# A decoder layer on one core: the first norm's result turned in blocks on VectorE and carried through DRAM instead of turned on TensorE

## The chip, the cores and the metric

The kernel runs on one core of a Trainium2 chip. The core has five engines that each work through their own queue in order: TensorE (PE, matrix products), VectorE (DVE), ScalarE (ACT), GpSimd (POOL) and SyncE (SP, which here only issues DMAs). The metric is the time of one execution on the device in microseconds (us); lower is better. Everything is computed in float32.

## The reference, cut to what matters

The input has 16 sequences of 512 tokens with 256 features. For each sequence the reference computes an attention layer and a feed-forward layer, each followed by a residual addition and a layer norm without gain.

```python
q = query @ wq + query @ Aq @ Bq * LORA_SCALE
k = query @ wk
v = query @ wv + query @ Av @ Bv * LORA_SCALE
# 16 heads of 16; rope on q and k; causal softmax of q k / 4; out = attn @ v
x = _layernorm(x + out @ wo)                     # the first norm
h = x @ W_exp + b_exp                            # 256 -> 1024, the expansion product
h = butterfly(h, up_weights, 1024)               # ten stages, linear
h = gelu(h + up_bias, approximate=False)
h = butterfly(h, down_weights, 1024)             # ten stages, linear
x = _layernorm(x + h @ W_con + b_con + down_bias)  # the second norm
```

The butterflies are linear, so the kernel folds them into the two weight matrices once, at the start.

## The kernel before, in words

A sequence is cut into four tiles of 128 tokens; the features into two chunks of 128. The heads of a chunk are worked on in groups, even and odd ones apart, which gives four "quads" for each sequence: (chunk 0, even), (chunk 0, odd), (chunk 1, even), (chunk 1, odd). Each quad takes five slots, so a sequence takes 20 slots (`per = 20`). A slot is the unit of the order written out by hand: for each slot the program emits first the attention work of the slot, then a list of other work (`others[s]`), then a list of work for the end of the slot (`holes[s]`). Every engine's queue has its instructions in exactly this order; nothing is reordered later.

The attention work of a slot. Two passes run over the scores, 15 slots apart. The first pass (`largest`, L421 on PE and L430 on DVE) computes scores and finds the largest of each row; the second (`weights`, L479 on PE, L493 on ACT and L497 on POOL) computes transposed scores with that maximum taken off, applies Exp on ACT and zeroes the masked part on POOL. In each slot PE computes score products of both passes into two score banks, pb and pa, of which there is one each: the next slot's score products may only write a bank when its readers are done. In slots of kind 0 to 3 (the slot's number modulo 5) pb holds the Exp's scores and pa the maxima's. In kind 4 each bank holds half of both: on pb the Exp is emitted before the maxima, on pa the maxima before the Exp. After the scores, PE multiplies finished weights with the values (`weigh`, po, L521) in slots of kind 0, 2 and 4; then come the others of the slot.

For the sequence that starts at slot s = 20 b, the other work lies at these slots (counted from s; slot 40 + n of one sequence is slot n of the sequence two later):

- load_xT at 0, load_x (the residual input z) at 9
- projections of the next sequence's q and k (`project`, pqk, L337) in the hole of slot 10, four products of 1.8 us each; their swap DMAs; rope on POOL (`turn`) and a copy with rows masked on ACT (`part`) in the slots after
- values (`project_v`, pvv, L383) at -3, -1, 4 and 14, the copy on ACT
- the division by the softmax's sums (`normalize`, L553 and L554 on DVE) at 27 to 31 and 36 to 40
- output projection (`project_out`, pwo, L559) at 41 and 42, with the residual addition (L567) and the norm's statistics (L577, L578) on DVE
- first norm: `spread` at 42 (L589 on DVE, then a power on POOL, L590), `offset` at 43 (L595 on DVE), `centre` at 44 (four ACT instructions, L602, z = z * scale + offset)
- `turn_x1` at 45: eight 128x128 transposes on PE (pt, L616), two copies to SBUF on DVE (x1T, L617), and the addition of the output biases to z on POOL (L621)
- expansion product (`hidden`, ph, L633) at 46 to 49, two of eight chunks a slot, copied out by ACT (L646) or DVE (L644)
- the Gelus of all eight chunks (`gelus`, L651) at the head of the hole of slot 50, between two loads of ACT's function table (Exp and Gelu use different tables), while PE works on the projections of slot 10 of the later sequence
- contraction (`contract`, py, L660) in eight halves at 51, 52, 53, 55, 56, 58, 60, 63, each second half followed by the residual addition (L668) and statistics on DVE
- second norm: `spread` at 63, `offset` at 67, `centre` at 68, store of the result at 68.

The attention's second pass of a sequence runs at its slots 15 to 34. The last two sequences have orders of their own, and sequence 13 has its last two hidden chunks in slot 50 with Gelu applied straight from PSUM. In slots 2 to 44 the folding of the butterflies runs beside the attention as a list of small tasks. z tiles are in three buffers, x1T in one, h in one. SP's queue takes the DMAs in order; an issue that waits for a semaphore holds up those behind it. The lines that carry the first norm's way from z to x1T:

```python
pt = bank(f"pt1_{b}_{c}", [P, NT, P])
for t in range(NT):
    nc.tensor.transpose(pt[:, t, :], zs[b][:, t, c * P : (c + 1) * P], ident)
nc.vector.tensor_copy(
    state["x1T", b][:, c, :], pt.rearrange("p t q -> p (t q)")
)
```

## Time and profile before

| what | value |
|---|---|
| median of 3 runs | 1359.33 us (1358.64 to 1360.84) |
| the profiled execution's own time | 1357.15 us |
| its span, first to last instruction | 1355.4 us |
| PE busy | 1320.3 us (97%) |
| DVE busy | 925.8 us (68%) |
| ACT busy | 707.3 us (52%) |
| POOL busy | 510.9 us (38%) |
| granted TensorE clock | 0.993 |

In the lines of a timeline the first number is the start in us from the span's start, the second the duration (of all, where several are merged: x8), then the engine, the line of the kernel, the operation, and output<-inputs. What stands in brackets at the end is how long the engine had been idle before, and what it waited for. In a table of stretches the busy time of PE, PE's weight loads, DVE, ACT and POOL stand in this order, then the granted clock. In the groups by line, the numbers after the bar are the busy time of all together and the mean ns of one; pipelined matmuls overlap, so that their sum of durations is larger than their busy time.

### The profile page before, as it was taken

The numbers are of one execution on the slowest core, as the hardware profiler recorded it, in microseconds if no ns is written. First come the engines' busy times: TensorE is split into PE (matmuls) and PEld (weight loads), VectorE is DVE, ScalarE is ACT, GpSimd is POOL, SyncE is SP. The second block draws the span as 40 slices with busy tenths as digits, with TensorE's granted clock in tenths as the row PEclk, the third lists the DMA queues.
The fourth block names the chain that finished last, engine by engine and source line by source line (L and its number), as shares of the span: only waits on it lengthen the run. The fifth ranks groups of instructions, "written<-read, shape, count | busy, mean of one in ns | idle before, by whom it ended". The sixth has DMA issues, their size and how long they took to land.

```text
span 1355.4 us, 23859 instructions
## 1 busy us (share of the span) xinstructions
PE 1320.3 (97%) x8728; PEld 702.5 (52%) x8728; DVE 925.8 (68%) x2949; ACT 707.3 (52%) x1079; POOL 510.9 (38%) x777
## 2 busy tenths in 40 slices
PE   8898999999999999999999999999999999998998
PEld 4453545455454545555454554545555454554555
DVE  4788757667685766758577685857768685776632
ACT  2575454454646445464645545464554546445643
POOL 3534215344251533425153352515335252531311
PEclk9998999999999999999999999999999999999999
DMA  5311010110102011010110101010110101000000
GB/s 172 120 45 45 22 59 30 40 45 30 68 30 74 30 41 45 30 67 30 67 35 31 57 30 68 30 60 30 40 60 30 68 30 55 30 27 32 30 12 31
DMA packets 45685, 63.49 MB, mean 47 GB/s; under 512 B 5752, under 2 KB 26232, under 8 KB 45568
## 3 DMA queue, kind: packets, MB, share of 16 engines
q1 hardware_dynamic: 41680, 56.42, 11.8%
q10 hardware_dynamic: 3888, 5.55, 1.3%
q8 instruction: 69, 1.13, 0.3%
q14 instruction: 48, 0.39, 0.1%
HBM read 23.40 MB, written 8.91 MB: 24 GB/s over the span
## 4 chain that ended last, share of the span: by engine, by line
PE 84%; DVE 11%; ACT 3%; issue 2%; DMA 0%; POOLq 0%; POOL 0%; DVEq 0%; SPq 0%; ACTq 0%
PE pb L479 19%; PE ph L633 17%; PE py L660 16%; PE po L521 10%; PE pqk L337 8%; DVE junk L430 5%; PE pvv L383 4%; PE pwo L559 3%; PE pa L421 3%; DVE bn L577 1%; PE pb L421 1%; PE pt L616 1%; ACT pT L493 1%; PE pa L479 1%; DVE z L567 1%
## 5 line engine op out<-in xcount | busy, mean ns | idle before, releaser
L430 DVE CUSTOM_DVE_ANT_0 junk<-pa,causal 128x384 bf16<-128x384 f32 (+2 forms) x878 | 438.3, 499 | 235.0 <-PE pa L421 176.1
L493 ACT ACTIVATE pT<-pb 128x1024 f32<-128x1024 f32 (+1 forms) x314 | 293.8, 936 | 377.3 <-PE pa L421 227.6
L497 POOL TENSOR_SCALAR_AFFINE_SELECT pT<-pT 128x256 f32<-128x256 f32 x512 | 202.5, 407 | 733.3 <-ACT pT L493 731.6
L479 PE MATMUL pb<-qz,kz 17*128 17x512 f32 (+2 forms) x1756 | 328.8, 473 | 16.1 <-ACT pT L493 12.1
L421 PE MATMUL pa<-kz,qz 32*128 32x384 f32 (+3 forms) x1756 | 329.2, 474 | 4.2 <-DVE mx L430 4.2
L660 PE MATMUL py<-wdn,h 128*128 128x256 f32 x1024 | 252.1, 391 | 0.0
L479 PEld LDWEIGHTS pb<-qz,kz 17*128 17x128 f32 (+1 forms) x1756 | 142.9, 183 | 179.5 <-issue 82.2
L633 PE MATMUL ph<-x1T,yb 128*128 128x512 f32 x512 | 235.8, 604 | 0.0
L660 PEld LDWEIGHTS py<-wdn,h 128*128 128x128 f32 x1024 | 185.1, 189 | 72.2 <-issue 36.2
L521 PE MATMUL po<-pT,vaug 128*32 128x512 f32 (+3 forms) x2048 | 179.5, 446 | 0.0
L633 PEld LDWEIGHTS ph<-x1T,yb 128*128 128x128 f32 x512 | 92.4, 189 | 122.3 <-issue 97.6
L421 PEld LDWEIGHTS pa<-kz,qz 32*128 32x128 f32 (+1 forms) x1756 | 143.7, 184 | 13.6 <-DVE mx L430 11.2
L553 DVE RECIPROCAL sums<-sums 128x128 f32<-128x128 f32 x128 | 121.1, 946 | 0.0
L337 PE MATMUL pqk<-xT,wqk 128*128 128x512 f32 x256 | 118.5, 613 | 0.0
L646 ACT COPY h<-ph 128x512 f32<-128x512 f32 x84 | 49.2, 585 | 123.2 <-PE ph L633 123.2
L521 PEld LDWEIGHTS po<-pT,vaug 128*32 128x32 f32 x2048 | 47.1, 109 | 102.3 <-issue 78.2
L430 DVE DVE_READ_ACCUMULATOR2_ANT mx<- 128x1 f32 x1024 | 84.5, 82 | 0.0
L337 PEld LDWEIGHTS pqk<-xT,wqk 128*128 128x128 f32 x256 | 48.0, 194 | 61.9 <-issue 57.4
L365 POOL TENSOR_TENSOR swap<-swap,rope_sb 128x512 f32<-128x512 f32 x62 | 79.6, 1283 | 0.0
L602 ACT ACTIVATE z<-z,norm 128x256 f32<-128x256 f32 x128 | 66.7, 589 | 24.6 <-DVE norm L595 24.5
L668 DVE TENSOR_TENSOR z<-py,z 128x256 f32<-128x256 f32 x64 | 27.1, 423 | 74.1 <-PE py L660 73.9
L430 DVE CUSTOM_DVE_ANT_0 junk<-pb,causal 128x256 bf16<-128x256 f32 (+3 forms) x146 | 63.6, 436 | 17.3 <-PE pa L421 4.0
(91 smaller groups left out, 1334.2 us busy)
## 6 DMA issues: line engine op xcount, KB each, us to landing
xT<-in_xT SPq DMA_DIRECT2D x16, 512.0 KB
swap<-qz SPq DMA_DIRECT2D x64, 128.0 KB
swap<-kz SPq DMA_DIRECT2D x64, 128.0 KB
z<-in_x SPq DMA_DIRECT2D x16, 512.0 KB
sums<-x SPq DMA_DIRECT2D x64, 128.0 KB
out_y<-z SPq DMA_DIRECT2D x15, 512.0 KB
x<-x SPq DMA_DIRECT2D x32, 128.0 KB
early<-in_wexpT ACTq DMA_DIRECT2D x1, 1028.0 KB
```

The lines of the kernel that those rows point to most:

```text
L337: nc.tensor.matmul(pq, wqk[:, d, e : e + P], xTs[b][:, d, :], start=(d == 0), stop=(d == NC - 1))
L365: engine.tensor_tensor(swap, swap, rope_sb[:, 1, :], ALU.mult)
L421: lambda i=i, rows=rows, at=at, n=n, t=t, ps=ps: nc.tensor.matmul(ps[:, i, at : at + n], q[rows, par, t * P : n], k_[rows, par, 0:n], star ...
L430: lambda i=i, at=at, n=n, t=t, g=g, ps=ps: nc.vector.tensor_tensor_reduce(out=junk[:, 0:n], in0=ps[:, i, at : at + n], in1=causal[:, T - n ...
L479: lambda i=i, rows=rows, at=at, n=n, k=block, ps=ps: nc.tensor.matmul(ps[:, i, at : at + n], kt[rows, par, k * P : (k + 1) * P], qt[rows, ...
L493: nc.scalar.activation(pT[:, heads, 0:n], ps[:, :, at : at + n], AF.Exp)
L497: nc.gpsimd.affine_select(out=diag, in_=diag, pattern=[[0, 2], [1, P]], compare_op=ALU.is_ge, fill=0.0, base=0, channel_multiplier=-1,)
L521: nc.tensor.matmul(po[HG * g : HG * (g + 1), k * P : T], vaugs[b % 2][:, k, NG * c + g, first : first + HG], pT[:, g, at : at + n], start= ...
L553: nc.vector.reciprocal(sums[:, ts], sums[:, ts])
L602: nc.scalar.activation(zs[b][:, t, :], zs[b][:, t, :], AF.Identity, bias=norm[:, 2, t : t + 1], scale=norm[:, 1, t : t + 1],)
L633: nc.tensor.matmul(ph, wup[:, c, hc * P : (hc + 1) * P], state["x1T", b][:, c, :], start=(c == 0), stop=(c == NC - 1),)
L660: nc.tensor.matmul(py, state["h", b][:, hc, t * P : (t + 1) * P], wdn[:, hc, :], start=(hc == 0), stop=(hc == NHC - 1),)
```

## The change

For the 14 sequences but the last two, the first norm's result is no longer turned on PE. `centre` moves from slot 44 to slot 43, behind `offset`. In slot 44, ahead of the other work of that slot, `turn_x1_by_blocks` has DVE transpose z in blocks of 32x32 (four instructions of 128x256), writes the blocks to a DRAM tile by four DMAs of 128 KB (pieces of 512 bytes), and reads x1T back by one DMA of 512 KB; all five are issued by SP. In x1T the tokens are then in another order, so that `hidden` reads its moving operand through an access pattern of 16 runs of 32 columns. POOL's addition of the output biases moves to slot 47. `hidden` moves to 48 to 51, the Gelus and the projections that accompany them to the hole of slot 52 (12), the contraction to 53, 55, 56, 58, 60, 63, 65, 66, the second norm to 66, 68, 69 with the store at 70. The next sequence's rope and part steps move by two slots with the projections, load_x moves from 9 to 20, and `normalize` of chunk 0 from 27, 28, 29, 31 to 29, 30, 31, 33. Sequence 13 loses its two fused chunks; the last sequence's four pvv all go to its slot 12. The folding's tasks are spread up to slot 46 instead of 44.

```diff
+    def turn_x1_by_blocks(b):
+        blocks = ring2.tile([P, D // HG, NT, HG], F32, tag="blocks", name=f"blocks_{b}", bufs=1)
+        for t in range(NT):
+            nc.vector.transpose(blocks[:, :, t, :], zs[b][:, t, :])
+        turned = dram.tile([D // HG, HG, NG, P], F32, tag="turned", name=f"turned_{b}")
+        for n in range(NG):
+            nc.sync.dma_start(
+                turned[:, :, n, :].rearrange("f j k -> j f k"),
+                blocks[HG * n : HG * (n + 1)].rearrange("j f t i -> j f (t i)"),
+            )
+        x1T = ring2.tile([P, NC, T], F32, tag="x1T", name=f"x1T_{b}", bufs=1)
+        nc.sync.dma_start(x1T, turned.rearrange("(c f) j n k -> (f j) c (n k)", c=NC))
+        state["x1T", b] = x1T.rearrange("p c (n t i) -> p c t n i", t=NT, i=HG)
...
-                state["x1T", b][:, c, :],
+                state["x1T", b][:, c],
...
-            at = {1: (-16, -11, -13, -9), B - 1: (-1, 4, 10, 10)}.get(b, (-3, -1, 4, 14))
+            at = {1: (-16, -11, -13, -9), B - 1: (12, 12, 12, 12)}.get(b, (-3, -1, 4, 14))
...
-            at = {0: (2, 5, 7, 10), 1: (3, 6, 8, 11)}.get(b, (10, 10, 10, 10))
+            at = {0: (2, 5, 7, 10), 1: (3, 6, 8, 11)}.get(b, (12, 12, 12, 12))
...
-                    add(turning + (6 if i == 3 else 4) + step, part, b + 1, side, c, step)
-        add(s + 9, load_x, b)
+                    add(turning + (6 if i > 1 else 4) + step, part, b + 1, side, c, step)
+        add(s + 20, load_x, b)
...
-                at = (27, 28, 29, 31) if c == 0 else (36, 37, 39, 40)
+                at = (29, 30, 31, 33) if c == 0 else (36, 37, 39, 40)
...
             add(s + 43, offset, 1, b)
-            add(s + 44, centre, 1, b)
+            add(s + 43, centre, 1, b)
+        if b + 2 == B:
             for c in range(NC):
-                add(s + 45 + (b + 2 == B), turn_x1, b, c)
+                add(s + 45, turn_x1, b, c)
         if b + 2 < B:
-            late = 2 * (b + 3 == B)
-            for hc in range(NHC - late):
-                add(s + 46 + hc // 2, hidden, b, hc)
-            holes.setdefault(s + 50, []).insert(0, lambda b=b, late=late: gelus(b, NHC - late))
-            for hc in range(NHC - late, NHC):
-                holes[s + 50].append(lambda b=b, hc=hc: hidden(b, hc, True))
+            others[s + 44].insert(0, lambda b=b: turn_x1_by_blocks(b))
+            add(s + 47, add_biases, b)
+            for hc in range(NHC):
+                add(s + 48 + hc // 2, hidden, b, hc)
+            holes.setdefault(s + 52, []).insert(0, lambda b=b: gelus(b))
+            at = (13, 15, 16, 18, 20, 23, 25, 26)
+            if b + 3 == B:
+                at = (13, 15, 16, 18, 20, 23, 24, 25)
             for t in range(NT):
                 for half in range(2):
-                    at = (11, 12, 13, 15, 16, 18, 20, 23)[2 * t + half]
-                    if b + 3 == B and t == NT - 1:
-                        at = (23, 25)[half]
-                    add(s + 40 + at, contract, b, t, half)
-            add(s + 63 + 2 * (b + 3 == B), spread, 2, b)
-            add(s + 67, offset, 2, b)
-            add(s + 68, centre, 2, b)
-            add(s + 68, store, b)
+                    add(s + 40 + at[2 * t + half], contract, b, t, half)
+            add(s + 40 + at[-1], spread, 2, b)
+            add(s + 68, offset, 2, b)
+            add(s + 69, centre, 2, b)
+            add(s + 70, store, b)
...
-    for s in range(behind, 2 * per + 5):
-        tasks_at[s] = len(first) + -(-len(second) * (s - behind + 1) // (2 * per + 5 - behind))
+    for s in range(behind, 2 * per + 7):
+        tasks_at[s] = len(first) + -(-len(second) * (s - behind + 1) // (2 * per + 7 - behind))
```

More of the change, by code (lines that the diff above doesn't have):

```diff
@@ L608, in centre, with add_biases @@
             )
+    def add_biases(b):
+        nc.gpsimd.tensor_tensor(
+            zs[b],
+            zs[b],
+            bias2[:, 0:1, :].to_broadcast([P, NT, D]),
+            ALU.add,
+        )
     def turn_x1(b, c):
@@ L620, in turn_x1 @@
         if c == NC - 1:
-            nc.gpsimd.tensor_tensor(
-                zs[b],
-                zs[b],
-                bias2[:, 0:1, :].to_broadcast([P, NT, D]),
-                ALU.add,
-            )
+            add_biases(b)
+    def turn_x1_by_blocks(b):
[7 more added lines that the diff above has]
+                blocks[HG * n : HG * (n + 1)].rearrange("j f t i -> j f (t i)"),
+            )
+        x1T = ring2.tile([P, NC, T], F32, tag="x1T", name=f"x1T_{b}", bufs=1)
+        nc.sync.dma_start(x1T, turned.rearrange("(c f) j n k -> (f j) c (n k)", c=NC))
+        state["x1T", b] = x1T.rearrange("p c (n t i) -> p c t n i", t=NT, i=HG)
     def hidden(b, hc, fused=False):
```

## The prediction

> **What bounds the kernel now.** I read the page first: busy shares, then the chain that ended last, then the two groups that the change removes, then the busy times by stretch.

> ```profile
> PE 1320.3 (97%) x8728; PEld 702.5 (52%) x8728; DVE 925.8 (68%) x2949; ACT 707.3 (52%) x1079; POOL 510.9 (38%) x777
> PE 84%; DVE 11%; ACT 3%; issue 2%; DMA 0%; POOLq 0%; POOL 0%; DVEq 0%; SPq 0%; ACTq 0%
> L616 PE MATMUL pt<-ident,z 128*128 128x128 f32 x128 | 17.6, 280 | 0.0
> 480.00:1195.00 715.00, 713.20 (x4835) 376.34 (x4834) 503.25 (x1618) 380.62 (x556) 284.43 (x423) 1.00 0.13 44
> ```

> PE is busy 713.20 of 715 us in the middle of the run: any work taken from PE there is time gained, and any new wait of PE is time lost at full price. So the question is which slots still give PE enough work to cover the release of the score banks pb and pa. Two stretches of the timeline show that. First, slots 43 to 45 of one sequence (slot 44 starts at 560.27, slot 45 at 563.90):

> ```profile
> 558.45 1.02 ACT L493 ACTIVATE pT<-pb 128x1024 f32<-128x1024 f32 x1 [2.92 <-PE pa L421]
> 560.46 0.42 DVE L668 TENSOR_TENSOR z<-py,z 128x256 f32<-128x256 f32 x1
> 561.80 0.15 DVE L595 SCALAR_TENSOR_TENSOR norm<-stats,norm 128x4 f32<-128x4 f32 x1
> 561.90 0.60 ACT L493 ACTIVATE pT<-pb 128x512 f32<-128x512 f32 x1 [2.42 <-PE pa L479]
> 562.79 0.60 ACT L493 ACTIVATE pT<-pa 128x512 f32<-128x512 f32 x1 [0.29 <-DVE mx L430]
> 563.28 2.06 ACT L602 ACTIVATE z<-z,norm 128x256 f32<-128x256 f32 x4
> 563.90 0.70 PE L479 MATMUL pb<-qz,kz 17*128 17x512 f32 x2
> 565.66 1.09 PE L616 MATMUL pt<-ident,z 128*128 128x128 f32 x8
> ```

> The first norm's centring (L602) stands behind both Exps of slot 44, so it delays nothing; its offset (L595) came 0.1 us before the first of them. The other place shows that on pb the Exp must end before the DVE maxima of the same bank start:

> ```profile
> 88.08 0.59 ACT L493 ACTIVATE pT<-pb 128x512 f32<-128x512 f32 x1
> 88.70 0.42 DVE L430 CUSTOM_DVE_ANT_0 junk<-pb,causal 128x256 bf16<-128x256 f32 x1 [0.35 <-ACT pT L493]
> 89.71 0.70 PE L479 MATMUL pb<-qz,kz 17*128 17x512 f32 x2 [1.29 <-ACT x L232]
> ```

> Second, near the end, a slot of kind 2 (the kind of slot 47) in which PE has only scores and po, then the next slot:

> ```profile
> 1249.83 0.59 PE L479 MATMUL pb<-qz,kz 17*128 17x384 f32 x2
> 1250.90 1.06 PE L521 MATMUL po<-pT,vaug 128*32 128x512 f32 x8
> 1252.16 0.92 PE L479 MATMUL pb<-qz,kz 17*128 17x384 f32 x4 [0.20 <-ACT pT L493]
> 1252.96 0.59 PE L421 MATMUL pa<-kz,qz 32*128 32x384 f32 x2
> 1254.02 1.99 PE L660 MATMUL py<-wdn,h 128*128 128x256 f32 x8
> ```

> From its start to the next slot's py: 4.19 us. The same kind with a pvv of 1.06 us in it (536.80 to 541.02) took 4.22. So a bare slot of this kind costs as much as one with 1.06 us of filler: 1.04 us of PE is lost (4.19 less 1.07 + 1.00 + 1.08 of work).

> **The change part by part.** 14 sequences take the new path.

> *Transposes off PE.* Eight pt take 565.66 to 566.68, 1.02 us; 14 x 1.02 = **-14.3**. [...]

> *Centring in slot 43.* In ACT's queue it now stands ahead of slot 44's Exps. It waits for the offset, which follows slot 43's py add, bn and aggregate on DVE; without the second norm's L589 ahead it comes 0.2 us sooner, 561.60 to 561.75. Centring then runs 561.8 to 563.8 and the Exp of pb starts at 563.8 instead of 561.90. From the Exp's start to PE's next pb took 1.63 us above (88.08 to 89.71), so slot 45 starts at 565.4 in place of 563.90: +1.5 for 13 sequences; the first has no py ahead of it, about +0.5. **+20.0**. Lower bound: only the Exp counts, 564.4 + 0.1, +0.6 each (+8); upper: 1.9 (+26). Queued behind the waiting centring are these Exps alone and the pvv copy.

> *Slot 47 bare.* py is now in slots 45 and 46, the product in 48 to 51, and nothing of PE in 47: +1.04, and slot 46's py is followed by add, bn, aggregate and L589 on DVE (0.42, 0.43, 0.18, 0.17), which starts 47's maxima some 0.1 us late. 14 x 1.1 = **+15.4** (0.9 to 1.3: 12.6 to 18).

> *DVE transposes.* Two copies (1.28 us together) go; four of 128x256 come. No row has one; nearest is another 128x256 f32 operation, 0.42, so 1.7 us, ending near 567.0 and followed by slot 45's maxima, done by 568.5; PE wants pa at 569.05 (565.4 + 1.19 + 0.57 + 1.92). Cost 0. Below nothing: 0, since DVE holds nothing else there. Far end: RECIPROCAL, 0.95 for 128 columns, so 7.6 us in all and a wait of 5.3 (+74). [...]

> *By way of DRAM.* SP issues four stores (0.55 each, as for swap), then the load, which waits for all.

> ```profile
> 501.74 0.38 SPq L672 DMA_DIRECT2D out_y<-z  x1
> 504.67 0.38 SPq L94 DMA_DIRECT2D z<-in_x  x1
> ```

> A 512 KB store here released its waiter in 2.9 us. So: 567.05 + 2.2 + 2.5 to 3 = 572.0, then some 3 us for the load: 575. hidden in slot 48 is wanted at 565.4 + 3.68 + 2.99 + 4.2 = 576.3. Hidden with 1.3 us to spare; each us later costs 14. Behind it on SP stand slot 45's sums and x (567.04 before, now about 572.6), read in slot 49, near 580. Nothing.

> *Strided moving operand* of ph, 32 columns at a time: nearest is DVE's every-second-element write, 426 ns for 423: 0, at most 4% of 206 us (+8).

> *One answer each.* POOL's biases (2.37) move from 45 to 47, next reader py adds in 53: 0; without that cover 2.4. Second offset, centring and store a slot or two later, beside 3.63 us of hidden: 0; without it as slot 44. load_x nine slots later, past a store it used to wait for, 21 slots ahead of its use: 0. Gelus in 52 beside four projections: ACT needs 2.3 + 7.57 + 1.02 = 10.9 to release slot 54, PE has 12.1 of work: 0. POOL's rope steps and ACT's part two slots later, done two slots before their reader: 0.

> *Head.* Sequence 0 has no py before it: slots 45 and 46 are bare too, 1.4 and 1.7 lost (maxima ready 3.15 and 2.75 after the start, work 1.76 and 1.07); the folding spread over 32 slots, not 30, gives some 0.6 back: **+2.5** (-1 to +5).

> *Tail.* pvv leaves 299 and 304 (+1.0, +1.06), hidden fills 309, bare before (-1.0), and the Gelus' slot 312 has 9.3 us of PE work under ACT's 10.9: 1.6 idle where 0.9 was: **+1.8** (0 to +4).

> Sum: -14.3 + 20.0 + 15.4 + 2.5 + 1.8 = **+25.4**. The profiled execution took 1357.15 (span 1355.4): 1382.5. The median, 1359.33, lies 2.2 above it: **1385**.

> **The rivals.**
> - *The banks come free in time* (faster). Place: first scores of slots 45 and 48. Before, PE lost 1.8 us in 715, so the order always had cover. Then only -14.3: 1345. It decides if the two waits together stay under 0.7 us a sequence. Against: the bare slot of 1249.83.
> - *Only slot 47 costs*: the offset comes early enough that centring falls into ACT's idle 2.42 us before 561.90. Against: the offset follows a py that ends at 560.27. 14 x (1.1 - 1.02 - 0.18) + 4.3 = +3: 1362.
> - *Slow turn or trip*: transposes nearer the reciprocal's rate, or 512-byte pieces landing 2 to 3 us later, so that slot 48's product waits: 1385 + 14 to 60, up to 1445. For: only 1.3 us of margin. Against: the 2.9 us store.

> **How the numbers follow.** Forecast 0.62 (own range 1374 to 1396); banks free 0.13; only slot 47 0.12; slow turn or trip 0.13. About 0.2% (2.7 us) is what a measurement can tell. Slower: 0.62 + 0.13 + 0.05 = 0.80; same 0.05; faster 0.15. The range leaves out the first rival and the top of the third: 1357 to 1412.

> **What would show it.** No L616 rows but two sequences'; L602 of the first norm between the Exps of slots 43 and 44 and PE's pb of slot 45 about 5.1 us after slot 44's first; slot 47 to slot 48's ph 4.2 us or more; PE idle some 2.7 us a sequence. Wrong if PE's busy share stays 97%, if ph waits for a DMA, or if a DVE transpose takes well over 0.42 us.

## The result and the profile after

The changed kernel takes 1401.48 us (median of 4, 1397.45 to 1404.47) against 1360.09 us before (median of 4): ratio 1.0314 [1.0283, 1.0345], slower by 41.4 us. The forecast was 1385 us, in a range of 1357 to 1412. The direction and the mechanism of the wait stand. The size was 16 us too small: 1401.5 lies outside the forecast's own 1374 to 1396, and is covered only by the wide range, whose upper part was there for a slow trip through DRAM, which is not what happened. Two things make up the difference: the granted clock, which the forecast did not have at all, and the head of the run, which it took too small. The profiled execution took 1404.47 us (span 1402.8), 47.3 more than the profiled one of before.

From the page of the changed kernel, its busy shares and the chain that ended last:

```profile
PE 1339.8 (96%) x8616; PEld 706.2 (50%) x8616; DVE 918.1 (65%) x2977; ACT 707.1 (50%) x1081; POOL 512.4 (37%) x777
PE 83%; DVE 8%; ACT 6%; issue 2%; DMA 1%; POOLq 0%; POOL 0%; SPq 0%; DVEq 0%
```

PE has 112 instructions fewer, and yet is busy for 19.5 us more. Taking instructions away cannot do that: the ones that are left must take longer (a py record took 391 ns on average before, 403 now). ACT's share of the chain rose from 3% to 6%. The middle of the run, as a table of stretches:

```profile
500.00:1235.00 735.00, 718.16 (x4754) 375.42 (x4746) 498.34 (x1636) 378.94 (x555) 284.86 (x423) 0.99 0.18 56
```

PE was idle for 1.8 us in 715 before, and is for 16.8 in 735 now; the granted clock, 1.00 there before, is 0.99. Where the idle time comes from, the waits of PE say (us in total, times, longest):

```profile
PE pb L479 <- ACT pT L493: 21.7, 31, 2.5
PE pb L479 <- ACT vaug L391: 17.3, 12, 1.4
```

The second row is new: twelve waits, one a sequence, 1.4 us each. It is put down to the last that ACT did in slot 44, a copy that ends at 583.43; what holds the bank is the Exp and the maxima behind it, whose last read ends at 583.60, 0.1 us before PE goes on. One of them in the timeline (sequence 5; slot 44 starts at 578.74, slot 45 at 583.70, slot 46 at 589.02, slot 47 at 592.01; this is the stretch that answers to 558.45 to 565.66 of before):

```profile
579.95 0.13 DVE L595 SCALAR_TENSOR_TENSOR norm<-stats,norm 128x4 f32<-128x4 f32 x1
580.11 2.08 ACT L602 ACTIVATE z<-z,norm 128x256 f32<-128x256 f32 x4 [2.17 <-DVE norm L595]
...
582.09 0.57 ACT L493 ACTIVATE pT<-pb 128x512 f32<-128x512 f32 x1
582.57 0.58 ACT L493 ACTIVATE pT<-pa 128x512 f32<-128x512 f32 x1
582.70 0.42 DVE L430 CUSTOM_DVE_ANT_0 junk<-pb,causal 128x256 bf16<-128x256 f32 x1 [1.55 <-ACT pT L493]
...
583.17 0.43 DVE L430 CUSTOM_DVE_ANT_0 junk<-pb,causal 128x256 bf16<-128x256 f32 x1
583.52 0.08 DVE L430 DVE_READ_ACCUMULATOR2_ANT mx<- 128x1 f32 x1
583.52 1.42 DVE L636 STREAM_TRANSPOSE blocks<-z 128x256 f32<-128x256 f32 x4
...
583.70 0.70 PE L479 MATMUL pb<-qz,kz 17*128 17x512 f32 x2 [1.44 <-ACT vaug L391]
...
584.96 1.89 SPq L639 DMA_DIRECT2D turned<-blocks  x4
...
585.71 3.38 PE L679 MATMUL py<-wdn,h 128*128 128x256 f32 x8
...
588.99 0.38 SPq L644 DMA_DIRECT2D x1T<-turned  x1
...
590.09 1.99 PE L679 MATMUL py<-wdn,h 128*128 128x256 f32 x8
...
594.35 0.91 PE L479 MATMUL pb<-qz,kz 17*128 17x384 f32 x4 [0.20 <-ACT pT L493]
...
595.21 0.59 PE L421 MATMUL pa<-kz,qz 32*128 32x384 f32 x2
...
596.28 1.13 PE L652 MATMUL ph<-x1T,yb 128*128 128x512 f32 x2
```

Read it downwards. The four centring instructions now stand ahead of the Exps, so the Exp of pb starts 3.35 us after slot 44's first product, not 1.63. The maxima of pb follow, and PE gets pb back 1.61 us after the Exp's start (1.63 in the stretch that the forecast used). PE stands still for 1.44 us. That much was forecast. Then look at the two rows of py, each half a contraction (four products; the trace holds 1024 records for the 512 products of the contraction, two each, hence x8): the same work takes 3.38 us at 585.71 and 1.99 at 590.09. The table of stretches shows why (granted clock: the third number from the end):

```profile
582.00:585.00 3.00, 1.56 (x14) 0.57 (x16) 2.21 (x9) 1.50 (x5) 2.05 (x3) 1.00 0.00 0
585.00:588.50 3.50, 3.50 (x15) 2.31 (x14) 1.39 (x4) 2.05 (x3) 0.41 (x1) 0.52 0.69 150
588.50:592.00 3.50, 3.50 (x19) 1.93 (x17) 1.40 (x4) 1.02 (x1) 0.41 (x1) 0.99 0.42 102
```

For some 3.4 us behind the wait (here from 585.14 to 588.55) TensorE was granted half of its clock (0.50 in just that stretch). This is the 1.65 us that slot 45 takes longer in 7 of the 14 sequences (2, 3, 5, 7, 9, 11 and 13); which waits are followed by it, the last section says. The starts of the slots' first products, taken from the two traces, give a sequence like this:

| from slot to slot, us | before | after | after, with the half clock |
|---|---|---|---|
| 44 to 45 | 3.64 | 4.96 | 4.96 |
| 45 to 46 | 2.78 | 3.68 (other work in it) | 5.32 |
| 46 to 47 | 4.70 | 3.00 | 3.00 |
| 47 to 48 | 5.70 | 2.34 | 2.34 |
| 44 to 64, the period | 79.54 | 81.00 | 82.65 |

And the whole difference of the two profiled executions, with two halves of sequence 0's contraction (py, 4.0 us of PE together) put back to where they stood before, since they now lie behind slot 64, and the same done for sequence 12's two at slot 304:

| stretch | forecast | measured | of it half clock |
|---|---|---|---|
| head, to slot 64 | +3.1 | +13.3 | see below |
| 12 periods, slots 64 to 304 | +19.0 | +27.8 | 9.9 (6 x 1.65) |
| tail, from slot 304 | +3.4 | +6.3 | 2.9 (1.65, and 1.26 after slot 334) |
| sum, of rounded terms | +25.5 | +47.4 | |

### The profile page after: what moved, and what is told of

Read it like the earlier page. It is cut to its first block, busy times and chain, and to the rows that moved or that the text cites. A ratio compares the mean times of both kernels' runs of the same rounds, so it can differ in the third digit from the quotient of the medians.

```text
span 1402.8 us, 23700 instructions
## 1 busy us (share of the span) xinstructions
PE 1339.8 (96%) x8616; PEld 706.2 (50%) x8616; DVE 918.1 (65%) x2977; ACT 707.1 (50%) x1081; POOL 512.4 (37%) x777
## 4 chain that ended last, share of the span: by engine, by line
PE 83%; DVE 8%; ACT 6%; issue 2%; DMA 1%; POOLq 0%; POOL 0%; SPq 0%; DVEq 0%
PE pb L479 19%; PE ph L652 17%; PE py L679 16%; PE po L521 9%; PE pqk L337 8%; PE pa L421 4%; DVE junk L430 4%; PE pwo L559 4%; PE pvv L383 3%; ACT pT L493 3%; ACT z L602 2%; DVE bn L577 1%; PE pb L421 1%; PE pd L267 1%; PE pa L479 1%
## 5 line engine op out<-in xcount | busy, mean ns | idle before, releaser
L430 DVE CUSTOM_DVE_ANT_0 junk<-pa,causal 128x384 bf16<-128x384 f32 (+2 forms) x878 | 438.3, 499 | 262.7 <-PE pa L421 199.6
L493 ACT ACTIVATE pT<-pb 128x1024 f32<-128x1024 f32 (+1 forms) x314 | 294.0, 936 | 393.8 <-PE pa L421 231.0
L479 PE MATMUL pb<-qz,kz 17*128 17x512 f32 (+2 forms) x1756 | 335.8, 479 | 42.6 <-ACT pT L493 21.7
L421 PE MATMUL pa<-kz,qz 32*128 32x384 f32 (+3 forms) x1756 | 332.8, 478 | 3.3 <-DVE mx L430 3.3
L679 PE MATMUL py<-wdn,h 128*128 128x256 f32 x1024 | 262.6, 403 | 0.0
L479 PEld LDWEIGHTS pb<-qz,kz 17*128 17x128 f32 (+1 forms) x1756 | 142.9, 185 | 210.3 <-issue 75.7
L679 PEld LDWEIGHTS py<-wdn,h 128*128 128x128 f32 x1024 | 192.2, 197 | 69.7 <-issue 41.6
L521 PE MATMUL po<-pT,vaug 128*32 128x512 f32 (+3 forms) x2048 | 182.3, 451 | 0.0
L421 PEld LDWEIGHTS pa<-kz,qz 32*128 32x128 f32 (+1 forms) x1756 | 144.8, 185 | 24.5 <-DVE mx L430 18.2
L521 PEld LDWEIGHTS po<-pT,vaug 128*32 128x32 f32 x2048 | 47.4, 109 | 102.9 <-issue 68.5
L602 ACT ACTIVATE z<-z,norm 128x256 f32<-128x256 f32 x128 | 66.9, 590 | 58.4 <-DVE norm L595 58.4
L430 DVE CUSTOM_DVE_ANT_0 junk<-pb,causal 128x256 bf16<-128x256 f32 (+3 forms) x146 | 63.6, 436 | 37.1 <-ACT pT L493 21.3
L430 DVE DVE_READ_ACCUMULATOR2_ANT mx<- 128x1 f32 x1024 | 84.6, 83 | 0.0
L590 POOL TENSOR_TENSOR norm<-norm,power 128x4 f32<-128x4 f32 (+1 forms) x38 | 35.1, 923 | 103.0 <-DVE norm L589 98.1
```

What stands on the lines that cost most here:

```text
L421: lambda i=i, rows=rows, at=at, n=n, t=t, ps=ps: nc.tensor.matmul(ps[:, i, at : at + n], q[rows, par, t * P : n], k_[rows, par, 0:n], star ...
L430: lambda i=i, at=at, n=n, t=t, g=g, ps=ps: nc.vector.tensor_tensor_reduce(out=junk[:, 0:n], in0=ps[:, i, at : at + n], in1=causal[:, T - n ...
L479: lambda i=i, rows=rows, at=at, n=n, k=block, ps=ps: nc.tensor.matmul(ps[:, i, at : at + n], kt[rows, par, k * P : (k + 1) * P], qt[rows, ...
L493: nc.scalar.activation(pT[:, heads, 0:n], ps[:, :, at : at + n], AF.Exp)
L521: nc.tensor.matmul(po[HG * g : HG * (g + 1), k * P : T], vaugs[b % 2][:, k, NG * c + g, first : first + HG], pT[:, g, at : at + n], start= ...
L602: nc.scalar.activation(zs[b][:, t, :], zs[b][:, t, :], AF.Identity, bias=norm[:, 2, t : t + 1], scale=norm[:, 1, t : t + 1],)
```

## The experiments

Ratios are against the kernel before, run beside each: 1359.42 us (median of 7) with the first four kernels, 1360.32 (23) with the next four, 1359.96 (12) with the last two.

### Centring back behind the Exps

The new kernel with the centring of slot 43 moved to slot 44, behind the Exps and right ahead of the block transposes. Theory: the wait and the half clock both come from the centring's place. Rival: the half clock comes from what else is new around slot 45.

```diff
-            add(s + 43, centre, 1, b)
+            if b + 2 == B:
+                add(s + 43, centre, 1, b)
...
             others[s + 44].insert(0, lambda b=b: turn_x1_by_blocks(b))
+            others[s + 44].insert(0, lambda b=b: centre(1, b))
```

> The changed kernel with one thing undone: for the 14 sequences of the new path the first norm's centring stands in slot 44 again, behind both Exps, with the turn in blocks right behind it. Theory A (PE waits for the score banks because the centring stands ahead of the Exps, and the wait brings the half clock): slot 44 to 45 falls from 4.96 to about 3.64 us in 13 sequences (-17), the 3.4 us stretches of half clock behind slot 45 go (7 of 1.65, -11), slot 47 stays bare (2.34 to slot 48): about 1401 - 28 = 1373. Rival B (the half clock comes from the added traffic or from the turn on VectorE, whatever the wait): only the -17, 1384, and half clock still behind slot 45.

Measured: 1375.12 us (1371.37 to 1380.37), 1.0126 [1.0092, 1.0161]. Slot 44 to 45 is 3.55 us, the period 79.60, and slot 45 is at the full clock in every one of the middle sequences (in sequence 5 its half contraction takes 1.99 us, for 3.38 in the changed kernel). One move, and 26 us of the 41 are gone. What is left, 79.60 against 79.54, says that all the rest of the change is worth nothing a sequence: the transposes' 1.02 us is lost again somewhere in it. The theory said 1373. One sequence (8) took 81.98; the trip through DRAM was late there, see below.

### Only the centring, on the kernel before

The opposite: the kernel before, with nothing but the centring one slot earlier.

```diff
-            add(s + 44, centre, 1, b)
+            add(s + 43, centre, 1, b)
```

> The kernel before with one part of the change alone: the centring of the first norm in slot 43, everything else as it was. Theory A: slot 44 to 45 goes from 3.64 to about 4.96 us in some 14 of 15 sequences (+18), and half-clock stretches of 3.4 us follow in about half of them (+11): 1360 + 18 to 30 = 1378 to 1390. Rival B: the order on ScalarE is covered by TensorE's work, 1360 to 1362, and the clock stays at 1.00 after the head.

Measured: 1399.48 us (1397.49 to 1407.46), 1.0314 [1.0276, 1.0352], the same ratio as the whole change, and above what was expected. In its timeline (slot 44 starts at 570.16):

```profile
571.70 0.15 DVE L595 SCALAR_TENSOR_TENSOR norm<-stats,norm 128x4 f32<-128x4 f32 x1
571.88 2.08 ACT L602 ACTIVATE z<-z,norm 128x256 f32<-128x256 f32 x4 [2.51 <-DVE norm L595]
...
573.87 0.58 ACT L493 ACTIVATE pT<-pb 128x512 f32<-128x512 f32 x1
...
575.48 0.73 PE L479 MATMUL pb<-qz,kz 17*128 17x512 f32 x2 [1.80 <-ACT vaug L391]
...
577.27 1.08 PE L521 MATMUL po<-pT,vaug 128*32 128x256 f32 x8
578.28 1.63 PE L616 MATMUL pt<-ident,z 128*128 128x128 f32 x8
```

The offset comes 1.54 us after slot 44's start here and 1.21 in the changed kernel, because here the second norm's L589 stands ahead of it. So slot 45 starts 1.68 us later than before (5.32 against 3.64), and 1.32 later in the changed kernel; the forecast's 1.5 lay between. The half clock follows the wait here too, without a block transpose or a trip through DRAM anywhere: eight transposes take 1.63 us where they took 1.02 to 1.09, and the granted clock was 0.59 from 575.40 to 578.90. One less the granted clock, summed from 240 to 1300 us of the span, is 17.1 us (before: 0.0). So the wait and the clock together are what the one moved line costs, and nothing new in the change is needed for either.

### Useless work into the wait

The changed kernel with two more products in slot 44 (x4 records), whose result nobody reads (this is the only kernel here that computes something beside the reference's work). Theory: the clock falls because of the idle time; then filling the wait, which is paid for anyway, must make the kernel faster. Rival: the clock answers to something else, and the extra work costs or is free.

```diff
+    def fill(b):
+        spare = bank(f"spare_{b}", [P, D])
+        for d in range(NC):
+            nc.tensor.matmul(
+                spare, xTs[b + 2][:, d, 0:P], wv_sb[:, d, :], start=(d == 0), stop=(d == NC - 1)
+            )
...
+            add(s + 44, fill, b)
```

> The changed kernel with work added: two products of the size of one pvv (1.06 us of TensorE) in slot 44, whose result nobody reads, so that TensorE works through most of its wait. Theory A: the wait itself ends when it did (slot 44 to 45 stays 4.96 us), the idle time before slot 45 falls from 1.44 to about 0.4 us, and the half-clock stretches behind it go: about 1401 - 11 = 1390, faster although 14.8 us of work were added. Rival B (half clock from traffic or from VectorE): no change, 1401; or, if TensorE is the bound there after all, 1415.

Measured: 1393.11 us (1391.31 to 1395.23), 1.0255 [1.0225, 1.0285], some 8 us below the changed kernel although it does more. Its waits of PE, and slot 44 and 45 of one sequence:

```profile
PE pb L479 <- ACT vaug L391: 6.9, 12, 0.6
```

```profile
659.57 1.13 PE L634 MATMUL spare<-wv_sb,xT 128*128 128x256 f32 x4
660.54 0.57 ACT L493 ACTIVATE pT<-pb 128x512 f32<-128x512 f32 x1
...
662.14 0.70 PE L479 MATMUL pb<-qz,kz 17*128 17x512 f32 x2 [0.58 <-ACT vaug L391]
```

Slot 44 to 45 is 4.96 us, exactly as in the changed kernel: the release of pb sets it, and 1.13 us more of PE work in front of it moves nothing. But the idle time fell from 1.4 to 0.6 us, and the period is 81.0 to 81.1 in all of sequences 1 to 12, none of which shows the half clock. Only sequence 13 does, and its wait is still 1.45 us long (1227.87 to 1229.31): its slot 44 has no values of a later sequence to project, so that the wait there was 2.50 us in the changed kernel. With the traffic and VectorE's work as they were, less idle time of PE took the half clock away; and the idle time was shown to come from the centring.

### Centring behind, and a contraction cut in three

The first experiment's kernel, with the last contraction tile's eight products dealt 2, 4, 2 over slots 45, 46 and 47, so that bare slot 47 gets work.

```diff
-            add(s + 40 + at[-1], spread, 2, b)
+            if apart:
+                for slot, first, stop in ((65, 0, 2), (66, 2, 6), (67, 6, 8)):
+                    add(s + slot, contract_some, b, NT - 1, first, stop)
+            add(s + 67 if apart else s + 40 + at[-1], spread, 2, b)
```

> The kernel with the centring in slot 44 and, besides, the last contraction tile's eight products spread as 2, 4 and 2 over slots 45, 46 and 47, where the change has 4, 4 and none. Theory A with the rule that a slot lasts for the longer of its work on PE and the release of the banks: slot 45 to 46 falls from 3.68 to about 2.85, slot 47 with 0.96 us of filler costs what the bare one did, so some 0.8 us less per sequence of 13: 1373 - 10 = 1363, within a few us of the kernel before on either side. If bare slots don't matter: 1373, as without the spreading.

Measured: 1368.75 us (1367.37 to 1369.4), 1.0075 [1.0052, 1.0099]. The period fell to 79.16, by half of what was hoped: slot 45 came down to 2.81 us, but 46 to 47 went up from 3.00 to 3.48. With less of PE's work in slot 45, slot 46 waits for the bank pa, whose maxima stand behind the block transposes on DVE: in one sequence these run from 571.01 to 572.93, the maxima end at 574.25, and PE's first product into pa follows at 574.31, 0.50 us after the first into pb. The trip was late here too, three times, 2.4 us together.

### The transposes back on PE, in the bare slot

The first experiment's kernel again, but turned as before: eight transposes on PE and two copies on DVE, now in slot 47; no blocks, no DRAM. If the bare slot of the new order costs what the transposes saved, they fit into it for nothing.

```diff
-            others[s + 44].insert(0, lambda b=b: turn_x1_by_blocks(b))
-            add(s + 47, add_biases, b)
+            others[s + 44].insert(0, lambda b=b: centre(1, b))
+            for c in range(NC):
+                add(s + 47, turn_x1, b, c)
```

> The kernel with the centring in slot 44, and the turn given back to TensorE: eight transposes and two VectorE copies in slot 47, no blocks, no trip through DRAM. Theory A (a slot lasts for the longer of TensorE's work and the release of the banks, and slot 47 was bare): the 1.02 us of transposes fit under the release, 47 to 48 goes from 2.34 to about 3.1 us while the end of slot 48's scores stays near 4.3 us after slot 47's start; the period 44 to 64 stays 79.6 us, or up to 0.4 more where the product waits for the copies: 1375 to 1381. If taking the transposes off TensorE was worth its 1.02 us: period 80.6, 1389.

Measured: 1371.77 us (1371.33 to 1372.6), 1.0085 [1.0062, 1.0109]. The period is 79.60, what it is without the transposes. Slot 47 of one sequence (it starts at 578.29):

```profile
579.37 1.06 PE L521 MATMUL po<-pT,vaug 128*32 128x512 f32 x8
...
580.36 1.09 PE L624 MATMUL pt<-ident,z 128*128 128x128 f32 x8
...
582.55 1.12 PE L652 MATMUL ph<-x1T,yb 128*128 128x512 f32 x2
```

From the start of slot 47 to the expansion product: 4.26 us with 1.09 us of transposes in it, 4.27 in the changed kernel without. So PE was relieved of work in a place where the score banks set the time. The first experiment's kernel, which goes by way of DRAM, had in its trace two sequences in which the trip came late (next experiment) and which were 2.6 us longer together; here there is none.

### A longer trip

The first experiment's kernel with the turned blocks copied once more from DRAM to DRAM before they are read.

```diff
+        again = dram.tile([D // HG, HG, NG, P], F32, tag="again", name=f"again_{b}")
+        nc.sync.dma_start(again, turned)
...
-        nc.sync.dma_start(x1T, turned.rearrange("(c f) j n k -> (f j) c (n k)", c=NC))
+        nc.sync.dma_start(x1T, again.rearrange("(c f) j n k -> (f j) c (n k)", c=NC))
```

> The kernel with the centring in slot 44, the trip through DRAM made longer by one more transfer of 512 KB from the first DRAM tile to a second, from which x1T is read. Between the issue of x1T's load and slot 48's product lay 4.5 to 7.4 us so far. Theory A (the trip is covered, with some 2 us to spare): a transfer more takes about 2.9 us, so slot 48's product waits 0 to 1 us: 1375 to 1389. If the trip already ends on TensorE's path (it would then share in the loss): 2.9 us for each of 14 sequences, 1416.

Measured: 1453.65 us (1444.49 to 1455.12), 1.0672 [1.0638, 1.0706]. Both expectations were far too low. Its waits of PE, and the trip in one sequence:

```profile
PE ph L654 <- DMA x1T<-again: 43.8, 14, 4.5
```

```profile
603.76 1.88 SPq L639 DMA_DIRECT2D turned<-blocks  x4
...
607.67 0.52 SPq L644 DMA_DIRECT2D again<-turned  x1
...
611.58 0.38 SPq L646 DMA_DIRECT2D x1T<-again  x1
...
615.95 2.93 PE L654 MATMUL ph<-x1T,yb 128*128 128x512 f32 x3 [3.13 <-DMA x1T<-again]
```

The legs can be read off the issues, each of which waits for the one before: the stores take 3.9 us from first issue to release, the copy 3.9, the load 4.4 until PE starts (3.8 to 4.4 in all sequences but one, which took 5.6). The forecast had 2.2 + 2.5 to 3 for the stores from the first issue, which is more than they take, and some 3 for the load, which is less. Hence the margin: in the changed kernel the product starts 7.3 us after the load's issue in the sequence shown, and 5.5 to 7.4 in all but one (4.3), so the trip mostly has 1.1 us or more to spare; but partly because the wait and the half clock push the product back. In the first experiment's kernel, with neither, it is 4.9 to 5.1 us in most, some 0.6 to spare, and in two sequences (3 and 8) the stores took 4.9 and 5.6 us and the product was late by 0.2 and 0.6 us. Behind the second of these the clock was halved too, and the sequence took 2.4 us longer. And in the kernel with the longer trip the half clock stands behind each of the 14 waits, which are 2.3 to 4.5 us long: the granted clock of the whole run is 0.951.

### The folding over its old slots

The kernel with the contraction cut in three, and the folding's tasks up to slot 44, as before the change, instead of 46.

```diff
-    for s in range(behind, 2 * per + 7):
-        tasks_at[s] = len(first) + -(-len(second) * (s - behind + 1) // (2 * per + 7 - behind))
+    for s in range(behind, 2 * per + 5):
+        tasks_at[s] = len(first) + -(-len(second) * (s - behind + 1) // (2 * per + 5 - behind))
```

> The kernel with the centring in slot 44 and the last tile's products spread as 2, 4, 2, and besides the folding's tasks spread over 30 slots as in the kernel before, not over 32. What it tells apart: the head of every kernel with the change is some 9 us longer up to slot 60 (236 to 238 us against 228). If the moved tasks do that (slot 28 takes 6.5 to 9.9 us for 3.0, with a fold product waiting in it): slot 60 at 228 to 231, total 1369 - 7 = 1362. If the later load of x, the later division or the bare slots 45 to 47 do it: slot 60 stays at 236 and the total at 1369.

Measured: 1366.07 us (median of 10), 1.0043 [1.0028, 1.0058]. Slot 28, which takes 8.2 us in the changed kernel and 9.9 with the contraction cut, at a granted clock of 0.79 and 0.65, takes 3.0 as before; slot 44 starts at 162.3 and not at 168.6 (before: 159.6). The clock is not all of slot 28's excess: in the first experiment's kernel it takes 6.5 us at the full clock. Two of these 6.3 us are given back at once: slots 47 and 48 of sequence 0, bare and behind idle time, now run at a clock of 0.67 and 0.70 (6.71 us for slot 48 where it was 5.61). So slot 60 comes at 232.2, between the two expectations, and the total does too.

### Two attempts at a faster kernel

The first one adds to the last kernel: the contraction dealt 3, 3, 2; sequence 13 on its path of before; the last sequence's pvv where they were.

```diff
+                for slot, first, stop in ((65, 0, 3), (66, 3, 6), (67, 6, 8)):
+                    add(s + slot, contract_some, b, NT - 1, first, stop)
...
+            if b + 3 >= B:
+                add(s + 44, centre, 1, b)
+                for c in range(NC):
+                    add(s + 45 + (b + 2 == B), turn_x1, b, c)
```

> What the runs so far point to: centring in slot 44, the folding over 30 slots, the last tile's eight products spread as 3, 3 and 2 over slots 45 to 47, and sequence 13 by the old path (transposes on TensorE in slot 45, product from slot 46), with the last sequence's values in the slots of before. Theory A: period 79.17 - 0.3 = 78.8 us for 79.54 before in eleven sequences (-7), the head as before but for some 3 us of bare slots, the tail as before: 1353 to 1360, faster than the kernel before by 0 to 0.5%.

Measured: 1363.24 us (1355.94 to 1366.79, 12 runs), 1.0019 [1.0003, 1.0034]: no gain, and above what was expected. The period is 78.83 where nothing disturbs it, but the product waited for the trip in four of the sequences, since the faster order wants it sooner:

```profile
PE ph L652 <- DMA x1T<-turned: 4.9, 4, 1.8
```

These four periods were longer by 1.3, 1.1, 0.8 and 3.6 us. So the trip was tried by itself: the first experiment's kernel with x1T read by four loads of 128 KB, each behind the store of its own part only, in place of one load behind all four.

```diff
-        nc.sync.dma_start(x1T, turned.rearrange("(c f) j n k -> (f j) c (n k)", c=NC))
+        for n in range(NG):
+            nc.sync.dma_start(
+                x1T[:, :, n * P : (n + 1) * P],
+                turned[:, :, n, :].rearrange("(c f) j k -> (f j) c k", c=NC),
+            )
```

> The kernel with the centring in slot 44, x1T read back by four loads of 128 KB, each behind its own store, in place of one load of 512 KB behind all four. The run with a longer trip showed that the one load takes about 4.2 us until TensorE can start, so that with the centring in slot 44 it lands 0.7 us or less ahead of need, and in two sequences (3 and 8) too late. Theory A: the last quarter lands about a microsecond earlier, no product waits for a transfer any more, period 79.60 in all of sequences 1 to 12: 1375 - 3 = 1372, as with the turn on TensorE. If smaller pieces or eight issues on SP take longer than the one load: waits of slot 48's product in more sequences, 1375 to 1385.

Measured: 1373.79 us (1370.86 to 1376.18), 1.0107 [1.0088, 1.0127]. No wait for x1T is left among PE's waits, and no sequence from 1 to 12 is longer than 79.74. The time alone does not tell it from one load (1375.12, 1371.37 to 1380.37); the missing waits do.

The second attempt has the four loads, and sends sequence 0, whose slots have no older sequence to fill them, by the path of before too, but for its last contraction tile.

```diff
+            if b == 0 or b + 3 >= B:
+                add(s + 44, centre, 1, b)
+                for c in range(NC):
+                    add(s + 45 + (b + 2 == B), turn_x1, b, c)
...
+            early_by = 2 * (b == 0)
+            if b > 0:
+                others[s + 44].insert(0, lambda b=b: turn_x1_by_blocks(b))
+                others[s + 44].insert(0, lambda b=b: centre(1, b))
+                add(s + 47, add_biases, b)
```

> The candidate of before (centring in slot 44, folding over 30 slots, last tile as 3, 3, 2, sequence 13 by the old path) with two more steps: x1T in four loads, and sequence 0 by the old path too, but for its last tile, so that the head is that of the kernel before up to slot 64. Theory A: period 78.8 us in sequences 1 to 12 without waits for a transfer (the candidate lost some 7 us by them), and no half clock at slots 47 and 48 of the head (4 us): 1363 - 11 = 1352, with 1348 to 1357 as what the head's clock can do to it; faster than the kernel before by 0.2 to 0.8%. If the loads in four are late too: 1358 to 1362, the same as before.

Measured: 1353.16 us (1348.83 to 1355.87, 7 runs), 0.9954 [0.9937, 0.9971]: faster than both kernels, by 6.8 us (0.5%) and by some 48, and where it was expected (1352). Its page:

```profile
PE 1319.8 (98%) x8632; PEld 700.2 (52%) x8632; DVE 940.0 (69%) x2973; ACT 705.0 (52%) x1079; POOL 508.9 (38%) x777
```

and its middle as a stretch:

```profile
242.00:1187.00 945.00, 941.90 (x6336) 494.24 (x6336) 686.20 (x2177) 506.14 (x742) 377.17 (x562) 1.00 0.18 58
```

PE is idle for 3.1 us in 945 and the clock is whole. The period is 78.82, 0.72 below before: of the 1.02 us of transposes, seven tenths arrive, once the centring stands behind the Exps and slots 45, 46 and 47 all have PE work to cover the banks. 12 x 0.72 is 8.6; in the profiled execution 7.3 of it shows between slots 64 and 304, and its head is 2.4 us later (slot 60 at 230.5, 228.1 before). Of its steps the centring, the contraction cut in three, the folding and the four loads were tried one at a time; the paths of sequences 0 and 13 and the dealing as 3, 3, 2 were not.

## Why the prediction was right in direction and short in size

- **Transposes off PE, -14.3, and slot 47 bare, +15.4.** Right, and right as a pair: with the centring out of the way the period is 79.60 against 79.54, and the transposes put back into slot 47 cost nothing. Slot 47 to the expansion product took 4.27 us (said: 4.2). What failed is the sentence ahead of the sum, that any work taken from a PE which is busy 713.20 of 715 us is time gained: with the transposes back in slot 47 the period stayed at 79.60. The bare slot also shows little as idle time (0.20 us at 594.35), since its score products are drawn out instead; so PE is idle for 1.9 us a sequence, and not for the 2.7 that were to show the forecast.
- **Centring in slot 43, +20.0.** The mechanism was right step by step (offset, centring, Exp, maxima, pb). Slot 45 starts 4.96 us after slot 44, not 5.1: +1.32 a sequence instead of +1.5.
- **The step that failed is the one behind it.** The forecast asked what was late next and stopped at pb. It priced the wait at its length and took the products behind it at their old durations. In half of the sequences those run at half the clock for 3.4 us, +1.65 each: 9.9 us in the middle, more than all other errors there, and 2.9 in the tail. No term of the sum, and no rival, had the clock in it.
- **Head, +2.5.** Mis-sized, +13.3 with sequence 0's own share against +3.1. From slot 44 on it holds: 3.2 us are lost between slots 44 and 60 (67.7 us against 68.5, with 4.0 of work less). The 10.1 us too much lie ahead of slot 44. The spread of the folding over 32 slots was booked as a gain of 0.6; undoing it, in the kernel with the contraction cut in three, brings slot 44 forward by 6.3. In the changed kernel slot 28 alone takes 5.2 us more than before. The rest is spread over the slots ahead of it; up to slot 17 it is some 3 us, and kernels of one order differ by as much there (41.9 to 44.9 us from slot 0 to slot 17).
- **Tail, +1.8.** About right: +6.3 with sequence 13's wait (1.3) and 2.9 of half clock leaves some 2.
- **DVE transposes, 0.42 each, cost 0.** Right:

```profile
L636 DVE STREAM_TRANSPOSE blocks<-z x56: 401/403/441, 174.9 to 1239.6; 128x256 f32<-128x256 f32 x56
L652 PE MATMUL ph<-x1T,yb x512: 592/592/697, 186.3 to 1382.9; 128*128 128x512 f32 x171
```

- **Strided moving operand, 0 to +8.** 0: the second row has min, median and max of ph in ns. The median is 592, as before.
- **By way of DRAM, hidden with 1.3 us to spare.** Right in outcome, since no wait for it is among PE's waits, but by two errors that cancel, which is luck: the stores were released about 4.0 us after their first issue, where 4.7 to 5.2 were said, and the load took 3.8 to 4.4 us (as the kernel with the longer trip shows), where 3 were said. In a kernel without the wait the margin was 0.6 us and was overdrawn at times, which the forecast's third rival had right in kind. (In the working for the DVE transposes, 565.4 + 1.19 + 0.57 + 1.92 is 569.08 and not 569.05; nothing rests on it.)
- **The rival that the banks come free in time** fell as the change stands. It comes nearest in the last kernel, by other orders than this change has, with 0.72 of the 1.02 us.

## What to carry to other kernels

An instruction taken off the busiest engine was worth its time here only in a slot where that engine's work is what lasts longest; price each slot as the longer of its work and the release of the next bank, and count what the move leaves bare (1.02 us of transposes went, and with the centring out of the way the period was 79.60 us for 79.54). A moved instruction that stands ahead of the one that releases a bank can cost more on its own than the whole of what it was moved for (here 1.3 to 1.7 us a sequence, for 1.02). And an idle stretch on TensorE was not priced at its length alone here (behind 1.44 us, 1.65 us more were lost in six of twelve sequences): look at the granted clock just behind existing waits of that size, and compare one product's duration there with its usual one.

## What the runs showed of the hardware

```profile
581.73:585.14 3.41, 1.97 (x18) 0.74 (x17) 2.35 (x9) 1.91 (x5) 2.05 (x3) 1.00 0.00 0
585.14:588.55 3.41, 3.41 (x15) 2.31 (x8) 1.25 (x4) 1.91 (x3) 0.41 (x1) 0.50 0.71 154
663.65:667.06 3.41, 1.97 (x23) 1.14 (x13) 1.82 (x9) 2.50 (x6) 2.20 (x4) 1.00 0.00 0
667.06:670.48 3.42, 3.42 (x28) 1.91 (x24) 2.00 (x6) 2.12 (x3) 0.94 (x2) 1.00 0.54 114
```

  That it is nearly every second sequence fits the grid too: a period of 81.00 us is 23.73 steps of the grid and one of 82.65 is 24.21, 47.95 together, so that every second wait lies at nearly the same place. What tells the two kinds apart within a step is not settled, since PE is busy for 1.97 or 1.98 us in all twelve; the steps that were followed hold more of the work behind the wait, which begins with the thin score products of 17 or 32 rows (1.26 to 1.97 us, for 0.51 to 1.06 in the others), and less of that ahead of it (0.01 to 0.72 us, for 0.91 to 1.46).
- In the kernel with the longer trip a 512 KB load from DRAM in pieces of 2 KB took 3.8 to 4.4 us (5.6 once) from its issue to the product that waited for it, and 512 KB from DRAM to DRAM took 3.7 to 4.1. Four stores of 128 KB took 3.9 to 4.3 us from first issue to the load's issue in 11 of the changed kernel's 14 sequences, and 4.7 to 5.5 in the other three, for a reason that stays open. Split into four loads, each behind its own store, the trip no longer held PE up: the two waits for x1T, 0.8 us together, were gone.
- The clock in slots 0 to 40, where the folding runs, differs from execution to execution of the same order: one less the granted clock, summed over these slots, is 15.4 to 22.2 us in the traces of the changed kernel and of six with the same order there (before: 6.8). What decides it was not settled, and that it is why the profiled executions differ by 47.3 us and the medians by 41.4 was not shown.
